# Conv-preact block on one core: the gate's last matmul moved behind the next pair's first shifts, and the second layer cut into half images

## The chip, the core and the metric

The kernel runs on one core of a Trainium2 chip. Its time is the device time of one execution in microseconds; the figure before the change is the median of three runs. Within the core, TensorE multiplies matrices, VectorE and ScalarE do elementwise work, GpSimd does some more, and SyncE (SP) issues most of the DMAs. ScalarE (ACT) can issue DMAs too, from its own queue.

## What is computed

The input has 32 images of 8 channels and 256 by 256 pixels, in f32. Two residual layers follow each other; `_gn` is a group norm over 4 groups of 2 channels.

```python
x = x + _L0_conv_ref(_gn(x), K_local, Wp, bp, Wu, bu, Wg1, bg1, Wg2, bg2)
x = x + _L1_conv_ref(_gn(x), weight, bias)

# layer 0, on a normalised x
grid = drive = x
for _ in range(15):
    mapped = 3.9 * grid * (1.0 - grid)
    local = conv3x3_depthwise(mapped, K_local)
    grid = 0.85 * (0.7 * mapped + 0.3 * local) + 0.15 * drive
cml_out = clip(grid, 0.0001, 1.0 - 0.0001)
nca_out = sigmoid(conv1x1(relu(conv3x3(x, Wp, bp)), Wu, bu))        # 128 hidden channels
gin = concatenate([x, cml_out, nca_out], axis=1)
g = sigmoid(conv1x1(relu(conv3x3(gin, Wg1, bg1)), Wg2, bg2))
out = g * cml_out + (1.0 - g) * nca_out

# layer 1, on a normalised x
sx, sw = 127 / max(abs(x)), 127 / max(abs(weight))
qx, qw = clip(round(x * sx), -127, 127), clip(round(weight * sw), -127, 127)
out = conv3x3(qx, qw) / (sx * sw) + bias
```

The scale `sx` needs the largest value of all images, so the second layer can start only when the first has finished the last image.

## The kernel before

**The first layer** takes the images in eight groups of four. Four kinds of work are written as Python generators and woven together: `lattice` (the 15 steps on the grid, matmuls at L511), `nca` (the hidden layer, L591 and L608), `gate` (L799 and L758) and `normalise`. `together` and `both` share out turns by the weights that the generators yield. TensorE keeps the order in which its instructions are written (`tc.manual_schedule` for that engine alone); on the other engines the planner sets the order. While the lattice of one group runs, the gate of the group before is woven into it. The gate of the last group has nothing beside it.

**The gate** works on an image in ten pairs of blocks. A block has 16 rows on the partitions, 8 channels each; 14 of the rows are results, so 19 blocks cover an image, and the tenth pair has one block. For a pair, `stage` loads the x, lattice and NCA inputs, `arrange` prepares the tiles `xnb`, `cmb` and `nb`, and 18 matmuls (three inputs, three column shifts, two halves of the output columns) sum into the PSUM tile `pa` (L799). ScalarE makes `r1` from it by a Relu (L812). `finish` then multiplies `r1` by the second weights (L758, into `pg`), takes the Sigmoid on ScalarE (L760), and on VectorE forms the new y (L762, L763) and its statistics (L771 to L773). `finish` of a pair is called at the head of the next pair's turn, before that pair's matmuls; the store of y waits for one more pair (L787).

**The second layer** (L936 to the end of the kernel function) loads an image of y at once (19 blocks, 2432 KB, four buffers), and works on whole images. VectorE subtracts the mean and scales (L978, three calls, since the rows outside the image in the first and last block need a scale of zero), rounds (L982), clips and casts to bf16 (L984, into `qt`, whose rows have a column of zeros on either side). TensorE makes three matmuls for each of ten pairs of blocks (L991); ScalarE scales each pair into `ob` (L992, two buffers). VectorE adds y (L995), and 19 DMAs store the blocks (L998). Loads are issued by SP for the first three images, by ScalarE for the others, three images ahead. In this part the planner sets the order on all engines.

Of the kernel before, what the change touches and what calls it, by code (L numbers as in the profile page):

```python
# [31 lines left out]
F32 = mybir.dt.float32  # L32
BF16 = mybir.dt.bfloat16
F32R = mybir.dt.float32r
AF = mybir.ActivationFunctionType
ALU = mybir.AluOpType
AX = mybir.AxisListType
DRAM = bass.MemoryType.DRAM
PSUM = bass.MemoryType.PSUM

P = 128
C = 8
# [4 lines left out]
MAX_Q = 127.0  # L47
ROUND = 1.5 * 2.0**23

NB = 19  # L50
STEP = 14
PW = W + 2
# [61 lines left out]
def kernel(  # L114
# [15 lines left out]
    nc = tc.nc  # L130
    B = x.shape[0]
    V, S, G, T = nc.vector, nc.scalar, nc.gpsimd, nc.tensor
# [8 lines left out]
    masks = cp.tile([P, 4], F32, name="masks")  # L141
# [11 lines left out]
    qw = cp.tile([P, 3, P], BF16, name="qw")  # L153
# [6 lines left out]
    mean_y = cp.tile([P, B], F32, name="mean_y")  # L160
    rstd_y = cp.tile([P, B], F32, name="rstd_y")
# [11 lines left out]
    with tc.tile_pool(name="prep", bufs=1) as pp, tc.tile_pool(name="prep2", bufs=2) as pp2:  # L173
# [24 lines left out]
        for t, n, w in (  # L198
# [3 lines left out]
            k = 64 if w == W else 43  # L202
# [63 lines left out]
    with ExitStack() as one:  # L266
# [4 lines left out]
        pool = lambda name, bufs, **kw: one.enter_context(  # L271
            tc.tile_pool(name=name, bufs=bufs, reuse_waits="tile", **kw)
        )
# [471 lines left out]
        def gate(b):  # L745
# [6 lines left out]
            def finish(p, r1, d, f):  # L752
                k0, n = 2 * p, (2 if p < 9 else 1)
                cols = n * W
                three = lambda t: t[:, :cols].rearrange("p (k w) -> p k w", w=W)
                pg = ps_c.tile([P, 512], F32, name="pg", tag="pt")
                for half in (slice(0, 64), slice(64, P)):
                    T.matmul(pg[half, :cols], gw2[:, half], r1[:, :cols], start=True, stop=True)  # L758
                gt = wk.tile([P, 512], F32, name="gate", tag="gate", bufs=3)
                S.activation(gt[:, :cols], pg[:, :cols], AF.Sigmoid, bias=bv[:, 1:2])  # L760
                y = gt
                V.tensor_tensor(three(y), three(gt), d[:, :n, :], ALU.mult)  # L762
                V.tensor_tensor(three(y), three(y), f[:, :n, :], ALU.add)  # L763
                rows = STEP if p < 9 else 4
                to_store = (
                    dram_ap(
                        y_s[b], (STEP * k0 + 1) * C * W, [[W, rows * C], [STEP * C * W, n], [1, W]]
                    ),
                    three(y)[C : C + rows * C],
                )  # L770
                V.bn_stats(st_a[:, p, :] if p < 9 else st_b, y[:, :cols])  # L771
                V.tensor_reduce(mx[:, p : p + 1], y[:, :cols], AX.X, ALU.max)
                V.tensor_reduce(mn[:, p : p + 1], y[:, :cols], AX.X, ALU.min)  # L773
                return to_store

            last = done = None
# [5 lines left out]
            for p in range(10):  # L782
                n = 2 if p < 9 else 1
                xnb, cmb, nb, d, f = ahead
                if last:
                    if done:
                        nc.sync.dma_start(*done)  # L787
                    done = finish(*last)
                pa = ps_a.tile([P, 512], F32, name="pa", tag="acc")
                three = pa[:, : n * W].rearrange("p (k w) -> p k w", w=W)  # L790
                i = 0
                for s, t in ((0, xnb), (1, cmb), (2, nb)):
                    if s == 2 and p < 9:
                        ahead = arrange(*ahead)
                    elif s == 2 and b + 1 in staged:
                        staged[b + 1] = staged[b + 1][0], arrange(*staged[b + 1][1])
                    for dx in range(3):
                        for half in (slice(0, 64), slice(64, P)):
                            T.matmul(  # L799
                                three[half], gw[:, s * 3 + dx, half], t[:, :n, dx : dx + W],  # L800
                                start=(i == 0), stop=(i == 8),
                            )
                        i += 1
                    if s == 0 and p < 9:
                        ahead = stage(b, p + 1, sc)
                    elif s == 0 and (b + 1) % GB:
                        staged[b + 1] = begin_gate(b + 1)
                    if s == 1 and sums:
                        sums.pop(0)()
                    if s == 2:  # L810
                        r1 = wk.tile([P, 512], F32, name="r1", tag="r1")
                        S.activation(r1[:, : n * W], pa[:, : n * W], AF.Relu, bias=bv[:, 0:1])  # L812
                        last = (p, r1, d, f)
                    yield 3.5 if s == 0 and p else 2.6
            if done:
                nc.sync.dma_start(*done)
            done = finish(*last)
# [101 lines left out]
        for g in range(NG):  # L919
            fill, t = images(nca, g), T_NCA  # L920
            if g:
                fill, t = both(fill, t, after(g - 1, images(gate, g - 1)), T_GATE), t + T_GATE
            if g + 1 < NG:
                fill, t = both(fill, t, prep(g + 1), T_PREP), t + T_PREP
            if g == 0:
                fill, t = chain(prep(0, ((1,), (2, 3))), fill), t + 30.0
# [9 lines left out]
    with ExitStack() as two:  # L936


        pool = lambda name, bufs, **kw: two.enter_context(
            tc.tile_pool(name=name, bufs=bufs, reuse_waits="tile", **kw)  # L940
        )
        tp, qp, op, sp, yp = pool("tp", 1), pool("qp", 2), pool("op", 2), pool("sp", 1), pool("yp", 4)
        ps = pool("ps", 4, space=PSUM)

        def load(b):
            y = yp.tile([P, NB, W], F32, name="yb", tag="yb")
            (nc.sync if b < 3 else nc.scalar).dma_start(
                y, dram_ap(y_s[b], 0, [[W, P], [STEP * C * W, NB], [1, W]])
            )
            return y  # L950

        ys = {b: load(b) for b in range(3)}

        gmax = sp.tile([P, 1], F32, name="gmax")
        V.tensor_reduce(gmax, dev_y, AX.X, ALU.max)
        gall = sp.tile([P, 1], F32, name="gall")
        G.partition_all_reduce(gall, gmax, P, bass.bass_isa.ReduceOp.max)
        sx = sp.tile([P, 1], F32, name="sx")
        V.reciprocal(sx, gall)
        V.tensor_scalar(sx, sx, MAX_Q, None, ALU.mult)  # L960
        inv = sp.tile([P, 1], F32, name="inv")
        V.tensor_tensor(inv, sx, sw, ALU.mult)
        V.reciprocal(inv, inv)
        qs = sp.tile([P, 3, B], F32, name="qs")
        V.tensor_scalar(qs[:, 0, :], rstd_y, sx, None, ALU.mult)
        V.tensor_scalar(qs[:, 1, :], qs[:, 0, :], masks[:, 2:3], None, ALU.mult)
        V.tensor_scalar(qs[:, 2, :], qs[:, 0, :], masks[:, 3:4], None, ALU.mult)
        qt = [qp.tile([P, NB, PW], BF16, name=f"qt{i}", tag=f"qt{i}", bufs=1) for i in range(2)]
        for t in qt:
            V.memset(t[:, :, 0], 0.0)  # L970
            V.memset(t[:, :, PW - 1], 0.0)

        for b in range(B):
            y = ys.pop(b)

            t = tp.tile([P, NB, W], F32, name="tq", tag="tq")
            for k0, k1, i in ((0, 1, 1), (1, NB - 1, 0), (NB - 1, NB, 2)):
                V.tensor_scalar(  # L978
                    t[:, k0:k1, :], y[:, k0:k1, :], mean_y[:, b : b + 1], qs[:, i, b : b + 1],
                    ALU.subtract, ALU.mult,  # L980
                )
            V.tensor_scalar(t, t, ROUND, ROUND, ALU.add, ALU.subtract)  # L982
            q = qt[b % 2]
            V.tensor_scalar(q[:, :, 1 : 1 + W], t, MAX_Q, -MAX_Q, ALU.min, ALU.max)  # L984
            o = op.tile([P, NB, W], F32, name="ob", tag="ob")
            for p in range(10):
                k0, n = 2 * p, (2 if p < 9 else 1)
                pt = ps.tile([P, 512], F32, name="pt2", tag="pt2")
                pt = pt[:, : n * W].rearrange("p (k w) -> p k w", w=W)
                for dx in range(3):  # L990
                    T.matmul(pt, qw[:, dx, :], q[:, k0 : k0 + n, dx : dx + W], start=(dx == 0), stop=(dx == 2))  # L991
                S.activation(o[:, k0 : k0 + n, :], pt, AF.Identity, bias=bv[:, 3:4], scale=inv)  # L992
            if b + 3 < B:
                ys[b + 3] = load(b + 3)
            V.tensor_tensor(o, o, y, ALU.add)  # L995
            for k in range(NB):
                rows = STEP if k < NB - 1 else 4
                nc.sync.dma_start(  # L998
                    dram_ap(out, b * C * H * W + STEP * k * W, [[W, rows], [H * W, C], [1, W]]),
                    o[C : C + rows * C, k, :],  # L1000
                )


# [43 lines left out]
```

## Time and profile before

| what | us |
|---|---|
| median of three runs (14065.71 to 14084.15) | 14070.34 |
| the profiled execution | 14065.15 |
| its span | 14063.3 |
| PE busy, whole span | 13110.3 |
| VectorE busy, whole span | 8273.9 |
| last lattice matmul issued at | 12881.0 |
| first load of the second layer issued at | 13284.24 |
| first scaling of the second layer begins at | 13300.35 |

The durations used below come from the one profiled execution, which is compared with its own time. In a group's line of the profile stand the source line, engine, operation, output and inputs with shapes, the count, then the busy time and the mean time of one in ns, then the time for which the engine stood idle before it and what ended that. In a chain, each line has a start, a length and what ran or was waited for. "SPq" and "ACTq" are the queues that issue DMAs. L numbers are lines of the kernel before.

### The profile page before, as it was taken

To read this page: it belongs to the slowest core of one execution; us is meant where nothing else is said; L and a number is where in the kernel's file an instruction comes from. 1 tells how busy PE (TensorE), PEld (TensorE's weight loads), DVE (VectorE), ACT (ScalarE), POOL (GpSimd) and SP (SyncE) were. 2 spreads that over 40 slices of the span, in tenths; PEclk is the share of its full clock that TensorE was granted. 3 is DMA by queue.
4 is the path that set the end of the run, shared out by engine and by line. 5 is a ranking of instruction groups with operands and counts; after the bars stand their busy time and mean duration, and the time that the engine had idled before them with its cause. 6 is when DMAs were issued, how large, how long until landed. Compare 5 with 4: busy or idle time off the path is not lost. (4 is left out here: it accounts for less than half of the span.)

```text
span 14063.3 us, 229517 instructions
## 1 busy us (share of the span) xinstructions
PE 13110.3 (93%) x81744; PEld 6304.1 (45%) x81744; DVE 8273.9 (59%) x16310; ACT 4036.2 (29%) x6274; POOL 2483.6 (18%) x4270
## 2 busy tenths in 40 slices
PE   5999999999999999999999999999999999999733
PEld 2444444444444444444444444444444444443211
DVE  5555555556556655566556656566556555555566
ACT  2233223222323232332223232332233222221132
POOL 1001111112111111111111211121112111112300
PEclk8999999999999999999999999999999999999966
DMA  6444444444444444444444444444444433333465
GB/s 150 96 103 97 91 108 106 114 94 104 106 110 97 102 105 105 103 103 102 108 100 105 109 99 100 110 107 97 101 108 112 98 81 87 87 84 79 124 188 179
DMA packets 2287208, 1496.74 MB, mean 106 GB/s; under 512 B 1096576, under 2 KB 2257152, under 8 KB 2285952
## 3 DMA queue, kind: packets, MB, share of 16 engines
q1 hardware_dynamic: 2210224, 1409.05, 42.8%
q10 hardware_dynamic: 75856, 73.02, 1.6%
q8 instruction: 664, 10.88, 0.3%
q14 instruction: 464, 3.80, 0.1%
HBM read 866.48 MB, written 478.69 MB: 96 GB/s over the span
## 5 line engine op out<-in xcount | busy, mean ns | idle before, releaser
L511 PE MATMUL pt<-m_a,lw 128*64 128x390 f32 x17280 | 5843.1, 496 | 157.1 <-DMA m_a<-m_a 109.3
L511 PE MATMUL pt<-m_b,lw 128*64 128x384 f32 x17280 | 5808.3, 491 | 18.8 <-DVE m_b L430 17.9
L601 ACT ACTIVATE h<-ph,bp_sb 128x512 f32<-128x512 f32 x4096 | 2585.1, 685 | 5283.9 <-PE ph L591 5209.8
L511 PEld LDWEIGHTS pt<-m_a,lw 128*64 128x64 f32 x17280 | 2298.1, 137 | 1795.2 <-issue 1633.3
L511 PEld LDWEIGHTS pt<-m_b,lw 128*64 128x64 f32 x17280 | 2304.3, 137 | 1649.5 <-issue 1550.6
L519 DVE SCALAR_TENSOR_TENSOR gt<-pt,d_a 128x384 f32<-128x384 f32 x2880 | 1581.5, 549 | 2005.2 <-PE pt L511 2005.0
L519 DVE SCALAR_TENSOR_TENSOR gt<-pt,d_b 128x390 f32<-128x390 f32 x2880 | 1607.0, 558 | 1939.0 <-PE pt L511 1936.4
L591 PE MATMUL ph<-im,wp_hi 48*128 48x512 f32 x12288 | 2621.1, 412 | 89.6 <-DMA im<-xp_s 59.0
L591 PE MATMUL ph<-im,wp_lo 48*128 48x512 f32 x12288 | 2509.9, 395 | 0.0
L528 POOL TENSOR_TENSOR m_b<-m_b,junk 128x12 f32<-128x12 f32 x2688 | 843.6, 314 | 8554.4 <-DVE m_b L524 8156.8
L591 PEld LDWEIGHTS ph<-im,wp_hi 48*128 48x128 f32 x12288 | 1239.8, 186 | 931.5 <-DVE m_b L524 185.8
L524 DVE SCALAR_TENSOR_TENSOR m_b<-gt 128x390 f32<-128x390 f32 x2688 | 1553.5, 578 | 47.0 <-DVE gt L519 0.5
L524 DVE SCALAR_TENSOR_TENSOR m_a<-gt 128x384 f32<-128x384 f32 x2688 | 1541.4, 573 | 18.1
L591 PEld LDWEIGHTS ph<-im,wp_lo 48*128 48x128 f32 x12288 | 1239.6, 186 | 229.9
L608 PE MATMUL acc<-h,wu_z 128*32 128x512 f32 x8320 | 1159.6, 600 | 6.5 <-ACT nca L626 5.5
L799 PE MATMUL pa<-cmb,gw 128*64 128x512 f32 (+1 forms) x3840 | 864.3, 580 | 14.8 <-POOL cmb L723 14.8
L799 PE MATMUL pa<-nb,gw 128*64 128x512 f32 (+1 forms) x3840 | 846.4, 573 | 0.0
L799 PE MATMUL pa<-xnb,gw 128*64 128x512 f32 (+1 forms) x3840 | 841.4, 571 | 0.0
L812 ACT ACTIVATE r<-pa,bv 128x512 f32<-128x512 f32 x320 | 213.2, 666 | 1758.0 <-PE pa L799 1757.9
L991 PE MATMUL pt<-qt,qw 128*128 128x512 bf16 (+1 forms) x960 | 270.9, 453 | 476.2 <-ACT ob L992 424.4
L729 DVE TENSOR_SCALAR xnb<-xb,sc 128x256 f32<-128x256 f32 x608 | 311.9, 528 | 578.0 <-DMA xb<-in_x_dram 569.8
L723 POOL COPY cmb<-cq 128x256 f32<-128x256 f32 x608 | 412.9, 706 | 915.5 <-DMA cq<-cm_s 775.6
(132 smaller groups left out, 7001.6 us busy)
## 6 DMA issues: line engine op xcount, KB each, us to landing
im<-xp_s SPq DMA_DIRECT2D x1152, 193.5 KB
im<-xp_s SPq DMA_DIRECT2D x1216, 96.8 KB
d_a<-xq_s SPq DMA_DIRECT2D x2048, 36.0 KB
nb<-nc_s SPq DMA_DIRECT2D x288, 256.0 KB
cq<-cm_s SPq DMA_DIRECT2D x288, 256.0 KB
yb<-y_s ACTq DMA_DIRECT2D x29, 2432.0 KB
xb<-in_x_dram SPq DMA_DIRECT2D x544, 128.0 KB
xp_s<-hi SPq DMA_DIRECT2D x256, 258.0 KB
```

What stands on the lines that cost most here:

```text
L511: T.matmul(pt[half], lw[:, c, k, half], beside if part == 2 else own, start=part < 2, stop=part > 0,)
L519: V.scalar_tensor_tensor(gt, pt, FLOOR, d[:, ts, :], ALU.max, ALU.add)
L524: V.scalar_tensor_tensor(to, gt, 1.0, gt, ALU.subtract, ALU.mult)
L528: G.tensor_tensor(edge, edge, junk.unsqueeze(1).to_broadcast([P, 6, 2]), ALU.mult)
L591: T.matmul(ph[:, :n].rearrange("p (h w) -> p h w", w=W), w[64 * i : 64 * i + 48, dx, :], rhs[:, :, dx : dx + W], start=(dx == 0 and w is w ...
L601: S.activation(h[:, :n], ph[:, :n], AF.Relu, bias=bp_sb)
L608: T.matmul(acc[32 * g : 32 * g + 32, :cols], wu_z[:, 24 - 8 * i : 56 - 8 * i], h, start=first, stop=last,)
L723: G.tensor_copy(cmb[:, k, 1 : 1 + W].rearrange("p (j q) -> p j q", q=4), cq[:, k, :].rearrange("p (q j) -> p j q", q=4),)
L729: V.tensor_scalar(xnb[:, k, 1 : 1 + W], xb[:, k, :], sc[:, i : i + 1], sc[:, 1:2], ALU.subtract, ALU.mult,)
L799: T.matmul(three[half], gw[:, s * 3 + dx, half], t[:, :n, dx : dx + W], start=(i == 0), stop=(i == 8),)
L812: S.activation(r1[:, : n * W], pa[:, : n * W], AF.Relu, bias=bv[:, 0:1])
L991: T.matmul(pt, qw[:, dx, :], q[:, k0 : k0 + n, dx : dx + W], start=(dx == 0), stop=(dx == 2))
```

## The change

In the gate, the call of `finish` for the pair before, with the DMA of the store before that, moves from the head of the turn to behind the first input's three column shifts.

In the second layer all engines now follow the written order. An image is worked in two halves of 10 and 9 blocks. All VectorE passes and the output tiles are per half; the quantising pass writes 10, then 8 and 1 blocks. Scaling and rounding are now two two-operation passes (`scaled`), and the upper clip is folded into the quantising pass. The rows outside the image are no longer scaled by zero; instead, the first and the last block are multiplied by copies of the weights whose rows for them are zero (`qwm`), so the first pair takes six matmuls. The add and the stores of an image come after the next image's quantising; 13 of the 19 stores are issued by SP and six by ScalarE, which then issues the load. PSUM has eight tiles instead of four, the output four half tiles instead of two whole ones.

```diff
@@ gate
-                if last:
-                    if done:
-                        nc.sync.dma_start(*done)
-                    done = finish(*last)
                 pa = ps_a.tile([P, 512], F32, name="pa", tag="acc")
...
                         i += 1
+                    if s == 0 and last:
+                        if done:
+                            nc.sync.dma_start(*done)
+                        done = finish(*last)
                     if s == 0 and p < 9:
                         ahead = stage(b, p + 1, sc)
@@ second layer
+        two.enter_context(tc.manual_schedule())
-        tp, qp, op, sp, yp = pool("tp", 1), pool("qp", 2), pool("op", 2), pool("sp", 1), pool("yp", 4)
-        ps = pool("ps", 4, space=PSUM)
+        tp, qp, op, sp, yp = pool("tp", 2), pool("qp", 1), pool("op", 4), pool("sp", 1), pool("yp", 4)
+        ps = pool("ps", 8, space=PSUM)
...
-            (nc.sync if b < 3 else nc.scalar).dma_start(
+            (nc.sync if b < 4 else nc.scalar).dma_start(
...
+        qwm = sp.tile([P, 2, 3, P], BF16, name="qwm")
+        for i in range(2):
+            V.tensor_scalar(qwm[:, i], qw, masks[:, 2 + i : 3 + i], None, ALU.mult)
+        qt = [[qp.tile([P, n, PW], BF16, name=f"qt{i}{j}") for j, n in enumerate((10, 9))] for i in range(2)]
+        for t in (*qt[0], *qt[1]):
+            G.memset(t[:, :, 0], 0.0)
+            G.memset(t[:, :, PW - 1], 0.0)
+        HALVES = ((0, 10), (10, NB))
+
+        def scaled(b, y, h):
+            h0, h1 = HALVES[h]
+            t = tp.tile([P, 10, W], F32, name="tq", tag="tq")[:, : h1 - h0, :]
+            V.tensor_scalar(
+                t, y[:, h0:h1, :], mean_y[:, b : b + 1], qs[:, b : b + 1], ALU.subtract, ALU.mult
+            )
+            V.tensor_scalar(t, t, ROUND, ROUND - MAX_Q, ALU.add, ALU.max)
+            return t
+
+        def quantised(b, t, h):
+            for k0, k1 in ((0, 10),) if h == 0 else ((0, 8), (8, 9)):
                 V.tensor_scalar(
+                    qt[b % 2][h][:, k0:k1, 1 : 1 + W], t[:, k0:k1, :], ROUND + MAX_Q, ROUND,
+                    ALU.min, ALU.subtract,
                 )
+
+        def convolved(b, h):
+            h0, h1 = HALVES[h]
+            o = op.tile([P, 10, W], F32, name="ob", tag="ob")
+            for k0 in range(0, h1 - h0, 2):
+                n = min(2, h1 - h0 - k0)
...
+                runs = [(0, n, qw)]
+                if h0 + k0 == 0:
+                    runs = [(0, 1, qwm[:, 0]), (1, n, qw)]
+                elif h0 + k0 == NB - 1:
+                    runs = [(0, 1, qwm[:, 1])]
+                for i, j, w in runs:
+                    for dx in range(3):
+                        T.matmul(
+                            pt[:, i:j, :], w[:, dx, :],
+                            qt[b % 2][h][:, k0 + i : k0 + j, dx : dx + W],
+                            start=(dx == 0), stop=(dx == 2),
+                        )
                 S.activation(o[:, k0 : k0 + n, :], pt, AF.Identity, bias=bv[:, 3:4], scale=inv)
+            return o
...
+        last = None
+        for b in range(B + 1):
+            if b < B:
+                y = ys[b]
+                ts = [scaled(b, y, h) for h in range(2)]
+                for h in range(2):
+                    quantised(b, ts[h], h)
+            if last:
+                i, os_ = last
+                yi = ys.pop(i)
+                for h, (h0, h1) in enumerate(HALVES):
+                    o = os_[h][:, : h1 - h0, :]
+                    V.tensor_tensor(o, o, yi[:, h0:h1, :], ALU.add)
+                store(nc.sync, i, os_[0], 0, range(0, 10))
+                store(nc.sync, i, os_[1], 1, range(10, 13))
+            done = last
+            if b < B:
+                last = b, [convolved(b, h) for h in range(2)]
+            if done:
+                i, os_ = done
+                store(nc.scalar, i, os_[1], 1, range(13, NB))
+                if i + 4 < B:
+                    ys[i + 4] = load(i + 4)
```

## The prediction

> **What bounds the kernel now.** I read the page first, for the shape of the run. (All times are us unless marked.)
>
> ```profile
> span 14063.3 us, 229517 instructions
> PE   5999999999999999999999999999999999999733
> PEclk8999999999999999999999999999999999999966
> DMA  6444444444444444444444444444444433333465
> ```
>
> TensorE is full until slice 37; then it falls to three tenths at a clock of 0.6, while the DMAs get busier. The windows cut there: the last four images' gate alone, the turn to the second layer, the second layer.
>
> ```profile
> 12881.00:13282.00 401.00, 351.43 (x1692) 118.71 (x1688) 191.90 (x391) 55.14 (x83) 161.39 (x166) 0.98 0.33 97
> 13300.30:14063.30 763.00, 270.95 (x960) 108.86 (x959) 519.92 (x193) 219.69 (x320) 0.00 (x0) 0.65 0.60 186
> ```
>
> The columns are length, busy PE, PE weight loads, VectorE, ScalarE, GpSimd, clock, DMA share, GB/s. In the second layer no engine is over 68% (VectorE, 519.92 of 763). So it is bound by a wait. Which one: the groups by form, SP's waits and the chain.
>
> ```profile
> L992 ACT ACTIVATE ob<-pt,bv,inv 128x512 f32<-128x512 f32 x288 | 205.1, 778 | 533.2 <-DMA out_dram<-ob 478.4 <-PE pt L991 50.1
> L984 DVE TENSOR_SCALAR qt<-tq 128x4864 bf16<-128x4864 f32 x32 | 167.1, 5221 | 123.0 <-PE pt L991 121.4
> L995 DVE TENSOR_TENSOR ob<-ob,yb 128x4864 f32<-128x4864 f32 x32 | 167.1, 5221 | 95.9 <-ACT ob L992 76.9 <-DMA out_dram<-ob 19.0
> L982 DVE TENSOR_SCALAR tq<-tq 128x4864 f32<-128x4864 f32 x32 | 86.2, 2694 | 1.1
> L978 DVE TENSOR_SCALAR tq<-yb,mean_y,qs 128x4352 f32<-128x4352 f32 x32 | 81.3, 2540 | 0.0
> L978 DVE TENSOR_SCALAR tq<-yb,mean_y,qs 128x256 f32<-128x256 f32 x64 | 26.1, 408 | 0.7
> ```
>
> ```profile
> SPq L998 <- DMA yb<-y_s: 124.5, 26, 12.0
> ```
>
> ```profile
> 13425.75 9.29 DMA yb<-y_s
> ...
> 13435.05 0.82 SPq L998
> ...
> 13435.97 0.81 SPq L998
> 13436.78 0.05 issue
> ...
> 13442.21 6.46 DMA out_dram<-ob
> ```
>
> ScalarE waits 478.4 for stores of ob to land: both output buffers are held by the stores. All 608 stores (19 an image) go through SP, at 0.82 each and about 0.9 from one to the next (13435.05, 13435.97, 13436.84): 17.0 an image. At the end, with no load running, the rate is the same (76 stores in 67.62 in the timeline, 0.89). SP also waits for loads: 124.5 in 26 waits, though no store reads a load. The chain shows one: load issued at 13425.75, landed 9.29 later, the next store 0.02 after that. In the trace the landings fall on eight semaphores in turn, so the eighth DMA after a load waits for it. From the first store (13330.80) to the end (14063.3) the layer takes 732.5, or 22.9 an image: 17.0 of issue, 3.9 of waits for loads, the rest waits for the add.
>
> In the gate-only stretch TensorE paces, with a hole per pair:
>
> ```profile
> 13253.11 2.75 PE L799 MATMUL pa<-nb,gw 128*64 128x512 f32 x12
> 13256.70 1.08 PE L758 MATMUL pg<-r,gw 128*64 128x512 f32 x4 [0.85 <-ACT r L812]
> 13257.61 2.74 PE L799 MATMUL pa<-xnb,gw 128*64 128x512 f32 x12
> ```
>
> pg needs the Relu (0.69 on ScalarE), which needs the pair's last matmul. pg comes every 9.65; its 40 matmuls at the spacing 2.57 per 12 are 8.6. The hole is 1.0.
>
> **What the Trainium skill says.** "VectorE: DVE Perf Modes", section "Mode 2×_2P": a one-source op in SBUF does two elements a cycle if the outermost non-unit dimension is even. The trace agrees: qt is written as 19 strided rows and takes 5221 ns for 4864 elements, one each 1.04 ns; the cast below goes to strided rows too, but of even number, and takes 670 for 1024.
>
> ```profile
> L376 DVE CAST hi<-xr x128: 670/689/696, 41.9 to 11165.5; 128x1024 fp32r<-128x1024 f32 x128
> ```
>
> "DMA: Bandwidth & Descriptors", section "Issuing engines are not separate DMA queues": a second issuing engine saves only the sequencer's time, "usually small relative to the DMA itself". Here that time is the bound: 112 KB each 0.9 is about 127 GB/s, while loads alone reach 342 (13427 to 13434). "TensorE: Matmul & The Clock Gate", section "What's actually happening": idle for a few us halves the clock; the windows show 0.50 at each image's start. So TensorE's busy time will not shrink.
>
> **The change, part by part.** Sums are against the profiled execution, 14065.15 (span 14063.3); the median 14070.34 lies 5 above.
>
> *Gate.* Nothing is added; pg moves past six or twelve matmuls (three shifts, two halves), so Relu has 2.57 to finish in, not none. In the stretch after 12881, 4 images have 9 such pairs each (the tenth keeps its wait): 36 × 1.0 = 36. With it move the Sigmoid, five VectorE operations (3.4), and on SP the earlier pair's store, still ahead of the next stage's loads. Those loads have room: xb for two pairs on landed at 12923.9, used at 12937. After that TensorE still paces: VectorE has 4.8 a pair (191.90 over 40) and GpSimd 4.0 (161.39 over 40). In the mixed stage before, pg waited for Relu 24.3 in 26 waits: possible gain 24. Possible loss: the five VectorE operations now fall into the lattice's next step. TensorE waits for the lattice's exchange 46.5 today; doubling that is a fair ceiling. Between −24 and +46 I take 0, for the Sigmoid and its followers sit in the same piece of filler work.
>
> *VectorE, second layer, an image.* Fixed part and rate from the rows: L978 4352 in 2540 and 256 in 408 give 0.52 ns an element plus 275; L982 gives 160 plus the same rate. Scale: 1.61 + 1.48. Round: 1.49 + 1.36. Quantise in 10, 8 and 1 blocks at the fast rate: 1.49 + 1.23 + 0.3 = 3.0 (5.5 if it stays slow). Add, at the slow rate in two halves: 2.82 + 2.55. Sum 14.3 against 16.5 today, with gaps 14.5.
>
> *ScalarE, an image.* Ten activations at their spacing of 0.66: 6.6. New: six stores at 0.9 and the load's 0.37. Sum 12.4; on this queue the next image's activations stand behind the stores.
>
> *SP, an image.* 13 stores × 0.9 = 11.7. No longer the bound.
>
> *DMA.* In the layer the two queues have 32.3% and 28.1% of 763 (DMA view), 14.4 an image. "DMA: Bandwidth & Descriptors", section "Why a DMA increments its semaphore by 16 and not by 1", lets a DMA use the largest number of engines up to 16 that divides both sides' slowest dimension: 14 for a store of 14 rows. No view shows which engines ran; counted so, the stores' part grows by 16/14 and the sum is 15.5, in which the engines would never rest, though loads alone overlap to a share of 1.03.
>
> *The loop of DMA semaphores.* Twenty DMAs an image in the written order: 13 SP stores, six ACT stores, the load. The eighth DMA after a load is the next image's eighth SP store, so it waits for the landing, 9.3 alone, 10 with a few stores beside it. Then four more SP stores (3.6), the twelfth's landing (2.2, as the chain shows without a load), and the next load, which by its place waits for that twelfth, may go. Period 10 + 3.6 + 2.2 = 15.8, say 16. This is what comes late next, just above VectorE and DMA. Output buffers (four halves, two images deep) and y (four) have over one period of slack.
>
> *Small items.* Three matmuls more an image (33), 0.2 in all, under TensorE's 8.5 busy of 16. Eight memsets go to GpSimd, at most 0.5 each by its memset of 512 elements, behind the first 5.9 of scaling. Two weight products on VectorE for two of qs: +0.3 once. The fourth load on SP hides before 13312, as today's on ScalarE.
>
> *Sum.* Scaling starts at 13300.4 as before. The first add is ready after two images' quantising (18) and one half add (2.8): first store 13321, against 13330.8. Then 28 periods of 16, three without loads at 14.5, and 14 for the last image's stores: 13826.5, which is 237 less. With the gate's 36: 273. 14065 − 273 = 13792; in medians 13797, forecast 13795.
>
> **Rivals.** (1) VectorE alone paces at 14.5: loads land in 8 or the semaphores fall otherwise. End 13321 + 31 × 14.5 + 14 = 13784.5, with the gate 315 less: 13755. For it: its sum stands closest. Against it: DMA would be full throughout. (2) The loop is longer: a store beside a load lands 6.46 after issue, as in the chain, and the load takes 12 as the longest wait does. Period 19: end 13910, with the gate 189 less: 13881. For it: both are in the trace. Against it: in the written order stores and load mostly alternate. (3) The quantising stays slow: VectorE 17, period 17 to the end: 13321 + 31 × 17 + 14 = 13862, with the gate 237 less: 13833. Against it: the cast row. (4) The other side: in the mixed stage the late pg makes VectorE late for the lattice, the exchange lands late, TensorE stalls. 284 pairs lie there; from 1.0 each it eats all 273. At 1.2: 14070 − 273 + 341 = 14138. Against it: VectorE is 59% busy and TensorE waits only some 120 of 11181 there.
>
> **How the numbers follow.** Chances: forecast 0.53, VectorE 0.17, long loop 0.18, slow quantising 0.06, lattice 0.04, something else, half of it near no change, 0.02. Range: the low end is rival 1 with the mixed stage's 24 too, 13730, and a little; the high end is rival 2 with 25 of mixed-stage loss: 13715 to 13905. A measurement here can tell 0.2% (28) from no change. Faster 0.94, same 0.02, slower 0.04.
>
> **What would show it.** Right: pg spacing near 8.6 after 12881, no wait for r; qt rows at 1.5 and 1.2; first to last store near 500; SP waiting for yb once an image, about 15.8 apart. Wrong: VectorE without idle time in the layer (rival 1); ScalarE waiting long for ob's stores (rival 2); a longer mixed stage (rival 4).

## The result, and the profile after

The changed kernel takes 13863.98 us against 14077.24 for the kernel before in the same comparison, 213 less: a ratio of 0.9847, 95% interval 0.983 to 0.9864. The profiled execution has a span of 13862.1, 201.2 less than the 14063.3 of before. First the page of the kernel after, its span and the busy tenths in 40 slices:

```profile
span 13862.1 us, 229831 instructions
...
PE   4899999999999999999999999999999999999964
...
PEclk8999999999999999999999999999999999999986
DMA  6444444444444444444444444444444433333368
```

The stretch in which TensorE is not full has shrunk from over two slices to about one and a half, and the DMAs are busier in it. The windows of the gate-only tail and of the second layer (length; busy PE, weight loads, VectorE, ScalarE, GpSimd; clock, DMA share, GB/s):

```profile
12921.00:13292.00 371.00, 352.39 (x1738) 128.34 (x1734) 181.21 (x401) 55.80 (x84) 161.73 (x170) 0.98 0.37 106
13300.30:13862.10 561.80, 275.13 (x1056) 126.56 (x1056) 447.38 (x295) 211.44 (x320) 0.75 (x9) 0.69 0.82 260
```

The first window starts at 12921, not 12881: the tail is shorter and begins later. Four marks taken from the trace cut the 201.2 into its parts: the last exchange transfer of the lattice, the last pg, the first and the last store of the output.

| stage | before | after | difference |
|---|---|---|---|
| to the lattice's last exchange | 12871.3 | 12921.1 | +49.8 |
| from there to the last pg (gate-only tail) | 410.6 | 371.2 | −39.3 |
| last pg to first store | 48.9 | 37.1 | −11.8 |
| first to last store | 729.4 | 529.3 | −200.1 |

So the second layer gave 212, the gate's tail 39, and the mixed stage, which was expected to stay as it was, took 50 back. (After the last store another 0.3 was lost.) The 50 sets two single executions against each other and is rough: in five profiled runs that share the changed kernel's mixed stage, this one among them, the last exchange comes between 12900.4 and 12921.1. Experiment 1 measures the loss on one chip.

The tail in the timeline of TensorE (start, busy time, instructions):

```profile
13246.18 1.03 PE L758 MATMUL pg<-r,gw 128*64 128x512 f32 x4
...
13252.19 2.75 PE L795 MATMUL pa<-xnb,gw 128*64 128x512 f32 x12
13254.77 1.03 PE L758 MATMUL pg<-r,gw 128*64 128x512 f32 x4
```

pg comes every 8.59, and the idle time before it that stood in brackets is gone.

The second layer, VectorE's groups by form (busy, mean ns, idle time before them and what ended it), ScalarE's group and one line of SP's waits:

```profile
L1040 DVE TENSOR_TENSOR ob<-ob,yb 128x2560 f32<-128x2560 f32 x32 | 90.4, 2825 | 23.4 <-ACT ob L1015 23.4
...
L982 DVE TENSOR_SCALAR tq<-yb,mean_y,qs 128x2560 f32<-128x2560 f32 x32 | 51.6, 1612 | 57.9 <-DMA yb<-y_s 57.9
L985 DVE TENSOR_SCALAR tq<-tq 128x2560 f32<-128x2560 f32 x32 | 47.8, 1494 | 1.1
L991 DVE TENSOR_SCALAR qt<-tq 128x2560 bf16<-128x2560 f32 x32 | 47.7, 1490 | 0.0
...
L991 DVE TENSOR_SCALAR qt<-tq 128x2048 bf16<-128x2048 f32 x32 | 39.1, 1223 | 0.0
```

```profile
L1015 ACT ACTIVATE ob<-pt,bv,inv 128x512 f32<-128x512 f32 x288 | 196.9, 790 | 340.4 <-DMA out_dram<-ob 304.7 <-PE pt L1010 35.6
```

```profile
SPq L1021 <- DMA yb<-y_s: 17.2, 4, 5.1
```

The quantising, 5221 ns for an image's 19 rows at once before, now takes 1490 for 10 rows, 1223 for 8 and 292 for the last one. VectorE is busy 447 of 562; in most images it stops once for the load of y, 57.9 in 26 waits. ScalarE's idle time is put down to stores of ob. The chain of waits says what these stores were waiting for:

```profile
13536.33 11.52 DMA yb<-y_s
13547.93 0.83 ACTq L1021
13548.76 0.04 issue
13548.85 0.82 ACTq L1021
...
13552.41 0.68 ACTq L1021
13553.08 0.04 issue
13553.12 11.52 DMA yb<-y_s
13564.71 0.83 ACTq L1021
```

It is a ring on one queue. ScalarE issues a load; the next thing on its queue, behind ten activations, is the first of its six stores, and that goes 0.08 after the load has landed, though it reads nothing of it; the load itself takes 11.52. The six stores take 5.2, and then the next load is issued: 11.5 + 5.2 = 16.8. The program's list of instructions confirms the link. In it DMAHW0 to DMAHW7 are the eight semaphores that tell of a landing, and a transfer waits for the one before it on its own semaphore. The list deals them strictly in turn, but in its own order: from ScalarE's fifth load on, seven stores of SP follow a load, and then ScalarE's six alternate with SP's other six. So the eighth transfer after a load, the next one on its semaphore, is ScalarE's first store. (After the first four loads it is one of SP's; these are SP's four waits for y.) One load and ScalarE's next store have the same:

```
L948 DMACopy yb<-y_s_155 128x19x256 [waits DMAHW0_49]
...
L1021 DMACopy out_dram<-ob 14x8x256 [waits DMAHW0_49,DVE_49]
```

### The profile page after: what moved, and what is told of

Its sections match the earlier page's. It is cut to its first block, busy times and chain, and to the rows that moved or that the text cites. A ratio compares the mean times of both kernels' runs of the same rounds, so it can differ in the third digit from the quotient of the medians.

```text
span 13862.1 us, 229831 instructions
## 1 busy us (share of the span) xinstructions
PE 13134.4 (95%) x81840; PEld 6403.4 (46%) x81840; DVE 8176.8 (59%) x16402; ACT 4028.2 (29%) x6274; POOL 2454.7 (18%) x4278
## 3 DMA queue, kind: packets, MB, share of 16 engines
q1 hardware_dynamic: 2191360, 1392.13, 43.1%
## 4 chain that ended last, share of the span: by engine, by line
PE 81%; DMA 8%; SPq 4%; DVE 3%; issue 1%; ACTq 1%; ACT 0%; POOL 0%; POOLq 0%; DVEq 0%
PE pt L511 36%; PE ph L591 20%; PE pa L795 16%; PE acc L608 7%; DMA yb<-y_s 2%; PE pg L758 2%; DMA im<-xp_s 1%; DVE gt L519 1%; ACTq L1021 1%; DMA m_a<-m_a 1%; DMA xb<-in_x_dram 1%; DMA xp_s<-lo 1%; SPq L464 1%; SPq L569 1%; DVE m_a L524 1%
## 5 line engine op out<-in xcount | busy, mean ns | idle before, releaser
L591 PE MATMUL ph<-im,wp_hi 48*128 48x512 f32 x12288 | 2685.1, 415 | 119.0 <-DMA im<-xp_s 59.4
L591 PE MATMUL ph<-im,wp_lo 48*128 48x512 f32 x12288 | 2569.9, 398 | 0.0
L591 PEld LDWEIGHTS ph<-im,wp_hi 48*128 48x128 f32 x12288 | 1312.0, 187 | 969.7 <-DVE m_a L524 180.7
L591 PEld LDWEIGHTS ph<-im,wp_lo 48*128 48x128 f32 x12288 | 1309.2, 188 | 218.6
L795 PE MATMUL pa<-cmb,gw 128*64 128x512 f32 (+1 forms) x3840 | 861.4, 580 | 15.5 <-POOL cmb L723 15.5
L762 DVE TENSOR_TENSOR gate<-gate,d 128x512 f32<-128x512 f32 x320 | 218.3, 682 | 823.0 <-ACT gate L760 805.0
L760 ACT ACTIVATE gate<-pg,bv 128x512 f32<-128x512 f32 x320 | 213.2, 666 | 1519.1 <-PE pg L758 1508.1
```

What stands on the lines that cost most here:

```text
L591: T.matmul(ph[:, :n].rearrange("p (h w) -> p h w", w=W), w[64 * i : 64 * i + 48, dx, :], rhs[:, :, dx : dx + W], start=(dx == 0 and w is w ...
L795: T.matmul(three[half], gw[:, s * 3 + dx, half], t[:, :n, dx : dx + W], start=(i == 0), stop=(i == 8),)
```

## The experiments

Two questions: where the 50 of the mixed stage come from, and what sets 16.8 an image. Ratios are to the kernel before on the same chip; that kernel's median was 14093, 14075, 14065 and 14059 in the four comparisons, so ratios and same-chip runs are compared, not times across chips.

**1. The gate's move alone.** The kernel before, with `finish` moved as in the change; the old second layer.

> The kernel before with the move of finish alone; the second layer is the old one. Theory A: the move gives back about 40 us in the gate-only tail (first pg to last pg 364.7 before, 324.4 after) and costs about 50 us in the mixed stage, where the last lattice exchange transfer came 49.8 us later (12871.3 to 12921.1). Then this run is 0 to 20 us slower than before, about 14087, with that transfer again near 12921. Theory B: the 50 us in the mixed stage don't come from the move (chance, or an effect of the new second layer on the program ahead of it). Then the transfer stays near 12871 and the run is about 40 us faster than before, 14037.

14092.96 against 14093.46: ratio 1.0 (0.9992 to 1.0008). The tail took 370.8 from the last exchange to the last pg, 40 less than before; that exchange came at 12944.6, 45 later than in the next run on the same chip. The interval of the ratio is 11 wide to either side, so with 40 gained in the tail some 30 to 50 are lost ahead of it. The move is worth nothing as a whole: what it gains at the end it loses on the way. Theory A.

**2. The second layer alone.** The changed kernel with `finish` back at the head of the pair:

```diff
                 xnb, cmb, nb, d, f = ahead
+                if last:
+                    if done:
+                        nc.sync.dma_start(*done)
+                    done = finish(*last)
...
-                    if s == 0 and last:
-                        if done:
-                            nc.sync.dma_start(*done)
-                        done = finish(*last)
```

> The new second layer with the gate's finish in its old place. Theory A: 212 us faster than before (the second layer took 781.3 and takes 569.6), about 13865, as fast as the whole change; the last lattice exchange transfer near 12871. Theory B: the mixed stage is late with the new second layer also when the finish stands in its old place; then about 50 us less gain, 160 us faster than before, about 13915.

13876.83, ratio 0.9847 (0.9833 to 0.986), 217 less, the ratio of the whole change. The last exchange is at 12899.5. So the new second layer does not delay the mixed stage.

**3. Late only where the gate is alone.** Both places are kept, each for its images:

```diff
+                if last and b < B - GB:
...
-                    if s == 0 and last:
+                    if s == 0 and last and b >= B - GB:
```

> The whole change, but the finish stands behind the first three column shifts only in the last four images, which have no lattice work beside them; in the others it is in its old place. Theory A: the tail's 40 us are kept and the mixed stage's 50 us are not paid: about 252 us faster than before, 13825, 40 us faster than the changed kernel. Theory B: the mixed stage is as late as in the changed kernel, and the time is within 10 us of it, about 13864.

13841.35, ratio 0.9821 (0.9808 to 0.9834): 252 less. Last exchange 12896.8, tail 371.6. The gain of the tail can be had without the loss.

**4. VectorE's part later still.** `finish` keeps the matmul and the Sigmoid in the new place and hands back the VectorE operations, which are called one shift sum later:

```diff
+                return lambda: mixed(p, gt, d, f)
...
-                        done = finish(*last)
+                        half_done = finish(*last)
...
+                    if s == 1 and half_done:
+                        done, half_done = half_done(), None
```

> The changed kernel, in which the last matmul and the Sigmoid stand where the change put them, and VectorE's four or five operations on the pair stand one column-shift sum later, behind the Sigmoid's end. The output is the same. Theory A1: VectorE's queue stands in the mixed stage because it waits for the late Sigmoid (706.5 us in 204 waits after, 345.7 in 109 before), and the lattice's operations behind it are late. Then most of these waits go, the lattice's last exchange transfer comes near 12880, and the run is 30 to 50 us faster than the changed kernel, about 13825. Theory A2: what is late is the release of the xb buffers, and so the load of the next pair, for which VectorE's queue stands (9 us at 9290). Then moving the operations later makes it no better or worse: 13864 to 13890.

13846.35, ratio 0.9824 (0.9811 to 0.9838), 247 less, last exchange 12900.3: the loss is gone. But half of theory A1 fails: the waits for the Sigmoid have not gone. The waits between 1700 and 12850, in the changed kernel:

```profile
DVE gate L762 <- ACT gate L760: 700.8, 201, 8.6
...
PE ph L591 <- DVE gt L519: 43.1, 46, 2.2
```

and in this one:

```profile
DVE gate L768 <- ACT gate L760: 693.1, 200, 8.6
...
PE ph L591 <- DVE gt L519: 18.9, 21, 2.2
```

The wait for the Sigmoid is as long as in the changed kernel, and harmless. What has changed is the second line: TensorE's hidden-layer matmuls (ph) wait for a bank that VectorE's lattice operation (gt) has to empty. Where the gate is not moved it is shorter, too: 16.3 in 19 waits with the second layer alone, and in the kernel before

```profile
PE ph L591 <- DVE gt L519: 15.5, 19, 2.5
```

With the gate's move alone it is 43.5 in 47. One such place in the timeline of VectorE, changed kernel:

```profile
9290.40 0.53 DVE L729 TENSOR_SCALAR xnb<-xb,sc 128x256 f32<-128x256 f32 x1 [9.01 <-DMA xb<-in_x_dram]
9290.85 1.12 DVE L762 TENSOR_TENSOR gate<-gate,d 128x512 f32<-128x512 f32 x1
9291.94 0.41 DVE L729 TENSOR_SCALAR xnb<-xb,sc 128x256 f32<-128x256 f32 x1
9292.26 1.76 DVE L763 TENSOR_TENSOR gate<-gate,xb 128x512 f32<-128x512 f32 x1
9293.95 0.55 DVE L519 SCALAR_TENSOR_TENSOR gt<-pt,d_a 128x384 f32<-128x384 f32 x1
9294.42 0.68 DVE L771 BATCH_NORM_STATS2 st_a<-gate 128x6 f32<-128x512 f32 x1
9295.02 0.66 DVE L772 TENSOR_REDUCE mx<-gate 128x1 f32<-128x512 f32 x1
9295.60 0.67 DVE L773 TENSOR_REDUCE mn<-gate 128x1 f32<-128x512 f32 x1
9296.20 0.54 DVE L524 SCALAR_TENSOR_TENSOR m_a<-gt 128x384 f32<-128x384 f32 x1
9296.66 0.55 DVE L519 SCALAR_TENSOR_TENSOR gt<-pt,d_b 128x390 f32<-128x390 f32 x1
```

and with VectorE's part later:

```profile
9279.09 0.86 DVE L729 TENSOR_SCALAR xnb<-xb,sc 128x256 f32<-128x256 f32 x1 [8.47 <-DMA xb<-in_x_dram]
9279.87 0.68 DVE L768 TENSOR_TENSOR gate<-gate,d 128x512 f32<-128x512 f32 x1
9281.59 0.52 DVE L729 TENSOR_SCALAR xnb<-xb,sc 128x256 f32<-128x256 f32 x1 [1.04 <-DMA xb<-in_x_dram]
9282.03 0.54 DVE L519 SCALAR_TENSOR_TENSOR gt<-pt,d_a 128x384 f32<-128x384 f32 x1
9282.50 0.55 DVE L519 SCALAR_TENSOR_TENSOR gt<-pt,d_b 128x390 f32<-128x390 f32 x1
```

The load of xb comes late in both, and VectorE stands for it 9 or 8.5. In the changed kernel all five operations of the pair stand behind that wait, two of them ahead of the first gt and all ahead of the second: that one (d_b) starts 6.26 after VectorE goes on, here, with one of the five ahead of it, 3.41. In the second layer alone the five run from 9272.11 on, while the load is still on its way, and gt follows 0.33 after the scaling. So it is the place in VectorE's queue, behind the load and before the lattice, that costs.

This is one place; the traces as a whole agree. Between 1700 and 12850, a hidden-layer matmul starts more than 1 us after the matmul before it 38 times in the changed kernel (65.4 in all) and 25 times here (37.1). On the one chip of experiments 1 and 2 it is 42 times (69.0) with the gate's move alone and 23 times (35.8) with the second layer alone, which shows 33 of the 45. Counted over all starts up to the last exchange, short ones too, the hidden-layer matmuls take 63.5 longer with the gate's move alone and the lattice's own 16.5, while pg, which no longer waits, gives back 16.7 and the others the rest.

**5. The load ahead of ScalarE's stores.**

```diff
-                store(nc.scalar, i, os_[1], 1, range(13, NB))
                 if i + 4 < B:
                     ys[i + 4] = load(i + 4)
+                store(nc.scalar, i, os_[1], 1, range(13, NB))
```

> The changed kernel with the load of image b+4 issued on ScalarE's queue ahead of the six stores instead of behind them. Theory A: the period of the second layer is a loop on ScalarE's queue, load to landing 11.5 us, the first store that shares the load's semaphore, six stores in 5.2 us, next load: 16.8 in all. With the load ahead of the stores the 5.2 us are no longer in the loop: the period falls to what bounds next, VectorE's 14.3 or the DMA engines' 14.4 to 15.5, so some 1.5 to 2.3 us an image for 32 images: 45 to 75 us faster than the changed kernel, 13790 to 13820. Theory B: the DMA engines, at 266 GB/s in this stage, set 16.8 themselves; then the time stays within 15 us of the changed kernel.

A miss: 13928.81, ratio 0.9899 (0.9882 to 0.9915). By the ratios that is some 73 slower than the changed kernel; experiment 7, which ran on the same chip and is as fast as the changed kernel, is 65 faster. The period settles at about 20. The load's landing is no longer in the chain, but another ring is:

```profile
13517.56 3.63 DMA out_dram<-ob
13521.26 0.83 ACTq L1021
...
13527.23 2.79 ACT ob L1015 x4
13530.04 2.84 DVE ob L1040
13532.90 0.81 SPq L1021
```

ScalarE's first store now takes its turn on the semaphore of SP's sixth store and waits 3.63 for that to land; then six stores (5.3), the activations of the next half image (3.4), its add (2.8), SP's stores up to the sixth (4.6): 19.8, from 13517.56 to 13537.32. Moving one issue has changed which transfers share a semaphore, not the sharing.

**6. The loads on SP,** behind the image's 13 stores:

```diff
                 store(nc.sync, i, os_[1], 1, range(10, 13))
+                if i + 4 < B:
+                    ys[i + 4] = load(i + 4)
```

> The changed kernel with all loads of the second layer on SP's queue, behind the image's 13 stores; ScalarE issues only six stores. Theory A: ScalarE no longer waits for a load's landing in its own queue; SP's issue work becomes 13 x 0.9 + 0.9 = 12.6 us an image, below VectorE's 14.3, but SP's stores behind the load may meet the load's semaphore in turn: if they do, SP stands up to 11.5 us each image and the period is 11.5 + 11.7 = 23 us (+190 us); if they don't, 15 us and 50 us faster than the changed kernel. Theory B (the DMA engines set the 16.8): within 15 us of the changed kernel. A period near 23 would show the shared semaphore as the cause by itself, since neither bytes nor VectorE's work change.

13916.24, ratio 0.9887 (0.9873 to 0.9902), 52 slower than experiment 7 on the same chip. The mean period, here and below the time from first to last store over 31, is 18.8, and about 20 in the second half: between the two cases that were expected. SP is held in two ways: in the chain of waits a store goes 12.31 after the load issued at 13535.51, and in the image before it another waits 10.53 for a store that had been issued right behind a load. Neither ring nor bytes alone explain this; how the two kinds mix stays open.

**7. Odd block counts.** The quantising in 9 and 1 blocks and 9 blocks:

```diff
-            for k0, k1 in ((0, 10),) if h == 0 else ((0, 8), (8, 9)):
+            for k0, k1 in ((0, 9), (9, 10)) if h == 0 else ((0, 9),):
```

> The changed kernel with the third VectorE operation of the quantising split into 9 and 1 blocks and 9 blocks, instead of 10, 8 and 1[...]. VectorE's work for an image grows from 14.3 us by 0 to 2.5 us, to at most 16.8. Theory A (the loop on ScalarE's queue sets 16.8): within 20 us of the changed kernel. Theory C (VectorE sets the period, with the loads as its only gaps): the growth comes through whole, up to 80 us slower. If the three rows last as long as before, it tells only that the block count doesn't matter to this form.

13863.92, ratio 0.9852 (0.9837 to 0.9866): as the changed kernel. Yet the rows are slow, 1.06 more than the 10 rows' 1490 for 256 elements fewer:

```profile
L991 DVE TENSOR_SCALAR qt<-tq 128x2304 bf16<-128x2304 f32 x36 | 91.8, 2550 | 0.0
```

VectorE's work grew by 2.4 an image, its busy share from 82% to 93% (the windows from 13500 to 13600), and the ring hid it all. In the changed kernel VectorE was not the bound, and beside the ring the even block counts earned nothing.

**8. The loads on GpSimd's queue,** on top of experiment 4. The program's list gives such loads semaphores of their own kind (DMASW0 to DMASW7), which no store takes.

```diff
-            (nc.sync if b < 4 else nc.scalar).dma_start(
+            (nc.sync if b < 4 else nc.gpsimd).dma_start(
```

> As vector_later, with the loads of images 4 to 31 of the second layer issued on GpSimd's queue, which has nothing else to do there; its transfers complete on semaphores of their own, so no store of ScalarE or SP takes a semaphore on which a load is under way. Bytes, stores and VectorE's work are unchanged. Theory A: the 16.8 us of an image are load 11.5 plus six stores 5.2, tied together only by the shared semaphore; without it the period falls to VectorE's 14.3 to 14.5 or to the DMA engines' 14.4 to 15.5, 1.3 to 2.4 us an image: 40 to 75 us faster than vector_later, 13770 to 13805. Theory B: what sets 16.8 is the DMA engines at 266 GB/s, or ScalarE's wait for the release of the ob buffers: then within 15 us of vector_later, 13846. Slower than vector_later by over 15 us would mean that GpSimd's issue of a load is itself slower than ScalarE's 0.46 us plus its transfer's 11.5.

13788.37, ratio 0.9804 (0.979 to 0.9817), 276 less than before: the lowest ratio of all versions. By the ratios that is some 28 less than experiment 4 (0.9804 and 0.9824), but the intervals touch. In the layer itself, first to last store, it is 38: 493.6 against 531.9; but the profiled execution, 13761.14, is the fastest of its five and 27 below their median, so 38 is the favourable end. The sign is A's, the size below its 40 to 75.

That the ring is gone shows in the periods rather than in the sum. 15 of the 31 are 14.5, below the ring's 16.8, with VectorE at work all the time; most others lie between 15.3 and 19.5, and the mean is 15.9. Bytes and work are the same. The run changes one more thing, the packets of the loads, now 4 KB for 1 KB; but the loads land no sooner for it, 13.9 after their issue (median) against 11.5. And the DMA engines forbade no more than 16.8, for they move 284 GB/s here (the last figure) and 269 in the changed kernel (13400 to 13800):

```profile
13400.00:13700.00 300.00, 172.93 (x611) 72.70 (x610) 270.63 (x169) 123.08 (x185) 38.97 (x19) 0.71 0.87 284
```

So the ring was what held 16.8; how much its removal is worth in a typical execution is less sure.

**9. Six output buffers for four,** on top of 8, with `pool("op", 6)`; run with 10 and the changed kernel on one chip. First the changed kernel:

> The changed kernel as it is, on the chip of the next two runs, so that they can be set against it directly. Both theories: 0.9847 of before, as measured; second layer 530 us from first to last store, mean period 17.1.

13852.95, ratio 0.9853 (0.9839 to 0.9866); first to last store 527.9, mean period 17.0, as in the profile above.

> load_on_pool with six ob buffers instead of four. With the loads on GpSimd 15 of 31 images took VectorE's 14.5 us and the others up to 19.5; there ScalarE waited for the release of an ob buffer by its stores (157.1 us in 25 waits within 300 us) and VectorE for ScalarE. Theory A: the release of ob is the second limit behind the load's semaphore; six buffers take it away, the mean period falls from 15.9 to 14.5 to 14.8, and first to last store from 493.6 to 450 to 465: 30 to 45 us faster than load_on_pool. Theory B: the stores themselves are late, by SP's issue and the DMA engines; then more buffers only move the wait from ScalarE to SP, the mean stays above 15.5 and the time within 12 us of load_on_pool.

A falls, and it is no better than B: 13803.79, ratio 0.9814 (0.9801 to 0.9828). First to last store is 526.4, mean period 17.0: no shorter than in the changed kernel on the same chip; the 49 between the two lie nearly all ahead of the layer. The wait is not gone (between 13400 and 13700):

```profile
ACT ob L1023 <- DMA out_dram<-ob: 179.8, 17, 18.8
```

It was 157.1 in 25 waits with four buffers. ScalarE's six stores, 5.2 in the ring above, here stretch to 10.7 (13469.65 to 13480.4), with pauses for stores of SP on the same semaphores. The longest is for one that SP issued at 13471.64, just after a load (13470.21), and that lands only at 13478.7. So semaphores shared among the stores go on tying the two queues together when the loads have left them. The row names a store of ob as what ended the wait, but more buffers of ob don't shorten it.

**10. Odd block counts,** the edit of experiment 7, with the loads on GpSimd.

> load_on_pool with the block counts of odd_blocks, whose quantising rows took 2 x 2.55 + 0.29 us an image instead of 1.49 + 1.22 + 0.29: 2.39 us more VectorE work an image, which cost the changed kernel nothing. Theory A: with the load's semaphore gone VectorE sets the pace of the fast images; they go from 14.5 to 16.9, the mean from 15.9 to at least 17, and the time rises by 35 to 75 us over load_on_pool. Theory B: the stores set the mean of 15.9 and the fast images only wait elsewhere; then the rise stays below 20 us.

13815.58, ratio 0.9825 (0.9812 to 0.9839), by the ratios some 30 more than experiment 8, with intervals that touch: less than A's 35 to 75, more than B's 20. All periods but the first two and the last are 16.8 or 16.9, and VectorE does not rest:

```profile
13400.00:13700.00 300.00, 154.69 (x585) 67.42 (x584) 298.75 (x162) 118.68 (x180) 36.95 (x18) 0.71 0.84 272
```

298.75 of 300. The images that took 14.5 now take 2.4 more, 16.9: VectorE is their bound. The mean period rises by 1.1 only, to 17.0 from the 15.9 of experiment 8's fastest execution, for the other images had slack. On this chip the last exchange of runs 9 and 10 is at 12862.8 and 12868.2, that of the changed kernel at 12906.8: the remedy of experiment 4 once more, 39 to 44, and most of what these runs gain on the changed kernel.

## Why the prediction was right, and where it was off

The forecast of 13795 was 69 too low, the measured time inside the range. Step by step:

- *Gate, the tail.* 36 pairs at 1.0 were to give 36; it is 39.3. pg's spacing was to be 8.6 and is 8.59, and the wait for r is gone. That TensorE would still pace there held.
- *Gate, the mixed stage.* This step failed. "Between −24 and +46 I take 0, for the Sigmoid and its followers sit in the same piece of filler work": it measured some +40 to +50. The loss was named, the five VectorE operations before the lattice's next step, but priced by TensorE's wait for the exchange and taken as cancelled. The runs show it at another place: the operations come to stand behind VectorE's wait for xb, the lattice's gt behind them, and TensorE waits for gt to empty a bank (15.5 in 19 waits before, 43.1 in 46 after). That VectorE is 59% busy was no cover: the lattice's gt was queued behind a wait. Rival 4 had this sign, with 1.0 for each of 284 pairs as its point of decision; it was some 0.15.
- *VectorE, second layer.* Every row was right within 0.01, the quantising included: 1.490 and 1.223 for 1.49 and 1.23. The pace they give is not 14.5 but 13.8, for starts overlap the ends before them: the first four periods of the changed kernel, whose loads were issued ahead, are 13.8. What the Trainium skill states in "VectorE: DVE Perf Modes", section "Mode 2×_2P", on the outermost dimension agrees twice over with this case: 10 and 8 rows at the fast rate, 9 rows 2550 ns. (The 670 read for the cast is its minimum; the median is 689.) Rival 3 is refuted.
- *The loop of DMA semaphores.* That the landing of a load holds a store which shares its semaphore, and so the next load, was right and bound the layer, as experiments 7 and 8 show. Its path was wrong. "The eighth DMA after a load is the next image's eighth SP store" takes the order in which the kernel is written; in the program's list ScalarE's stores come in between, and from the fifth load on the eighth is ScalarE's first. In place of 10 + 3.6 + 2.2 stand 11.5 for the load, among stores, and 5.2 for six stores: only the first term exists, and that the sums, 16 and 16.8, lie so close is luck. The sign set down for it, SP waiting for yb once an image, came only for the first four loads. First to last store was to be near 500; it is 529.3. The layer gave 212 for 237.
- *Rivals 1 and 2.* VectorE alone is what comes next, in half of the images, once the loads have semaphores of their own. ScalarE's long wait for stores of ob, the sign set down for rival 2, appeared (304.7) and would have misled: it was the ring of the load, at a period of 17 and not 19. Buffers were not tried against it in the changed kernel; with the loads on GpSimd two more don't shorten it.
- *The sum.* 36 + 237 expected; 39 + 212 − 50 measured in the profiled execution. Nearly all of the error is the mixed stage and the 1 us in the period. Both went the same way, so nothing cancelled; the range was wide enough for both.

## What to carry to other kernels

Before an operation is moved on one engine, look at what its followers on the other engines will then be queued behind: operations that used to fill the wait for a load can end up after it, ahead of someone else's work. Where transfers share a few completion semaphores, keep a long load off those that short stores take, for instance by issuing it from a queue with its own, and look at what the stores still share; here reordering alone only changed the pairs. Work out the pairs from the program's list, not from the order in which the kernel is written. When a row says that an engine waits for a store, follow the chain once round before buying buffers.

## What the runs showed of the hardware

VectorE's rounding of 2560 elements, 1494 ns in the changed kernel, takes 2197 with the loads on GpSimd (mean of 19 between 13400 and 13700); that of 2304 keeps its 1360. GpSimd's timeline puts an issue of 2.05 across each slow one:

```profile
13500.02 2.05 POOL L956 DMA_DIRECT2D yb<-y_s  x1 [15.61 <-DVE ob L1048]
```

```profile
13501.17 2.20 DVE L993 TENSOR_SCALAR tq<-tq 128x2560 f32<-128x2560 f32 x1
13503.29 1.46 DVE L990 TENSOR_SCALAR tq<-yb,mean_y,qs 128x2304 f32<-128x2304 f32 x1
```

The Trainium skill, "SBUF — State Buffer", section "SBUF: two separate sides", has VectorE and GpSimd share a pair of ports that one of them holds for a whole instruction while the other waits; the 0.7 agree in sign and place (the two overlap by 0.9), but no run isolates the lock. The 0.7 are the difference between VectorE's 13.8 and the 14.5 of experiment 8, whose last full period, with no load left to issue, is 13.8 again. So the way round the ring has this price. The same page would explain the 1.12 and 1.76 of the gate's product and sum at 9290, which take 0.69 each with the second layer alone: GpSimd's operations run beside them there. It was not tried; those 1.5 are part of the 6.26 in experiment 4.
